# First layer of a four-layer network on one core: six causal turns in a context step, rows turned per tile, block counts within the last routing, the rare blocks' branch in front

## The chip, the cores and the metric

The kernel runs as one program on 1 NeuronCore of a Trainium2 chip. The metric is the device time of one execution in microseconds (us), as a median of several runs. Beside the timed runs one execution is profiled; every reading of the trace below is from that one.

The engines are called as the profile calls them: PE (TensorE) multiplies and transposes into PSUM, DVE (VectorE) and ACT (ScalarE) work on PSUM and SBUF, POOL (GpSimd) does small elementwise work and issues the indirect transfers, SP issues the plain transfers. Each engine works through its own queue in order.

## The reference, cut to what matters

The network has four layers, all in float32, for `x` of 16 sequences of 64 tokens of 256 features (1024 tokens, eight tiles of 128) and a context of 1024 tokens of 192 features for each sequence. Each layer is a cross-attention to the context, a second mixer, and a feed-forward part, each added to `x` after a layer norm. The change touches the first layer alone:

```
x = x + L0_xattn(_layernorm(x), ctx, ctx, ...)       # cross-attention, one head
x = x + L0_attn(_layernorm(x), w_qkv, ln_w, w_proj)  # causal self-attention, 16 heads of 16
x = x + L0_ffn(_layernorm(x), gate_w, w1, w2, w3, sw1, sw2, sw3)

def L0_ffn(x, ...):                # 8 experts, the two largest of each token
    scores = softmax(x @ gate_w.T)
    topk_w, topk_i = top_k(scores, 2)
    y = sum over the two experts of weight * (silu(x @ w1[e]) * (x @ w3[e])) @ w2[e]
    return y + (silu(x @ sw1) * (x @ sw3)) @ sw2      # the shared part, all tokens
```

## The kernel before, in words

**Cross-attention and causal attention together.** `L0_first` walks over the eight tiles of 128 tokens in context steps, `for n in range(NT + 2)`. In step n it does the scores of tile n against its two sequences' contexts (L338; softmax at L222 and L224), the transposes of the exponentials of tile n-1 (L234) and its weighted averages over the context (L349, called `averaged`), and the output of tile n-2 (`by_features` at L357 and L358, `output` with `add_to_x` at L88). The order of PE in this stage is written by hand (`manual_schedule` on PE); the order of the other engines is made by the tile scheduler.

Between those pieces stand calls of `attn.go()`, the causal turns. Each call moves every causal tile at work one `yield` further. A causal tile (`tile(i)`) is a generator of about twenty such pieces: norm (`os`), transpose and eviction (`hTs`, L178), q, k and v (L68 on `hTs`), transposes of q and k (L721), scores `sc` (L68), softmax (DVE L745, L751 and L754, POOL L752, ACT L753), transposes (L760), averages `o` (L782), `sel` and `yT`, projection and addition to `x`. A tile can begin when the cross-attention of that tile is done, three turns after the one before it, and when one of three rooms (buffers) is free; two more rooms come from the context buffers after the last step. In the kernel before there are four turns in a context step. What is left after the last step is done in a loop, `while attn.go(): next(shared, None)`, in which one piece of the shared expert part follows each turn.

**PSUM.** `misc` has two banks in rotation for nearly all small products, `t` two for transposes (and, in this stage, for the shared part's `gu`), and `sc` two double banks, used by the context scores, by the causal scores (two at a time) and by the causal averages `o`.

**Routing.** After two causal tiles, `routing(g)` for that pair goes into the queue `behind`, of which only the first is at work: two layer norms into `htok`, rows written to HBM (`keep_row`, L1155), transposes into `hT` (L178), gate product (`hT` with `gate_w`, L68), then `route`: softmax (L1100 is its exponential on ACT), two largest, ranks (`t_both`, `ahead`), places, and the products of `s_col` and `s_who` into the routing table.

**Experts.** `L0_ffn` first runs `block_experts` (it counts the blocks of 128 routed rows of each expert, computes the list of each block's rows and tokens, and loads `n_blocks` into registers of all engines) between the pieces of the fourth shared part, and then `some_blocks`. There are 23 blocks at most, and 18 are written as plain code (`few`); the other five stand in a branch, `with self.tc.If(self.n_blocks > few)`, behind the 18. In the profiled execution the branch's body is not run. A block gathers its expert's weights `wa` and `wb` and its tokens' rows `hb` with indirect transfers issued by POOL (L1399, three buffers each, the first three of each asked for ahead of the loop), transposes `hb` (L178), multiplies (L68 into `gu` and `po`), and writes its result to `ys` in HBM (L1420, and the transfer at L1421 issued by ACT).

**The next layer's start.** `L1_xattn` needs `ys`: for each tile POOL gathers two `back` tiles (L1399) and DVE adds them to `x` (L1408), and only then come norm and queries (`o` at L894, transposed at L178). Keys and values of the first context (L930 to L951) need none of it.

## Time and profile before

| what | value |
| --- | --- |
| median of the 3 timed runs | 2840.32 us (2838.4 to 2840.79) |
| the profiled execution's own time | 2832.74 us |
| its span, first to last instruction | 2830.9 us |
| mean granted PE clock | 0.964 |
| PE busy | 2601.9 us (92% of the span), 18116 instructions |
| DVE, ACT and POOL busy | 1401.8, 1005.9 and 311.4 us |
| first layer's stages in the profiled execution | start to 42.4 us; steps 2 to 8 from 42.4 to 143.4; the rest of causal attention, routing and shared part to 276.7; expert blocks to 424.0 |

A line of a timeline gives start, duration (us), engine, line and operation, output and inputs, shape, and the number of merged instructions; square brackets hold the engine's idle time before it and what ended that. A line of windows gives each engine's busy time in one stretch, then the granted PE clock as a share of full speed, the DMA engines' share and GB/s. A busy PE is not a PE at its peak: at a lower granted clock the same matmuls show as more busy time.

### The profile page before, as it was taken

Reading aid. Unit: us, or ns where it says so; the run is one execution under the profiler, and the core shown is the slowest. Engines: PE = TensorE matmul, PEld = TensorE weight load, DVE = VectorE, ACT = ScalarE, POOL = GpSimd, SP = SyncE. Lnnn points to the kernel's source line nnn. Section 1 sums busy time; section 2 is a strip of 40 time slices with the busy share of each in tenths; the row PEclk is TensorE's granted clock in tenths of the full one; section 3 lists DMA queues with packets and bytes.
Section 4 is the critical chain, followed back from the end, with each engine's and each line's share of the span. In section 5 each row is a group of like instructions: output and inputs, shape, how many; then the busy total and the mean of one; then the engine's idle time right before and its main releaser. Section 6 shows DMA issues by size and latency. Waiting matters only on the chain.

```text
span 2830.9 us, 44725 instructions
## 1 busy us (share of the span) xinstructions
PE 2601.9 (92%) x18116; PEld 1890.9 (67%) x18116; DVE 1401.8 (50%) x2825; ACT 1005.9 (36%) x2116; POOL 311.4 (11%) x429
## 2 busy tenths in 40 slices
PE   7887998999999898979999999798999998998998
PEld 3566894666666687856666676695666665666777
DVE  3565126666666643233434342423344756658692
ACT  2341223555555431223232222122235445545330
POOL 1121423000000112310101000201001000000000
PEclk9987998999999998989999999799999999999999
DMA  9602862001001015801111112463113213121210
GB/s 268 194 27 83 346 239 67 27 27 39 27 27 35 31 38 193 291 23 49 58 61 51 45 49 87 155 237 108 51 49 94 84 49 96 56 76 31 62 44 8
DMA packets 78156, 253.70 MB, mean 90 GB/s; under 512 B 14079, under 2 KB 25882, under 8 KB 68218
## 3 DMA queue, kind: packets, MB, share of 16 engines
q1 hardware_dynamic: 58490, 165.00, 18.3%
q0 software_dynamic: 13312, 80.28, 7.8%
q10 hardware_dynamic: 6144, 5.51, 0.6%
q8 instruction: 145, 2.38, 0.4%
q14 instruction: 65, 0.53, 0.1%
HBM read 233.80 MB, written 14.81 MB: 88 GB/s over the span
## 4 chain that ended last, share of the span: by engine, by line
PE 39%; DVE 9%; ACT 3%; DMA 2%; issue 2%; POOL 1%; SPq 1%; ACTq 0%; DVEq 0%; POOLq 0%
PE sc L506 9%; PE ps_h L68 5%; PE misc L542 4%; PE halves L68 3%; PE misc L68 3%; PE ps_t L520 3%; PE halves L542 2%; PE gu L68 2%; PE misc L537 2%; PE halves L2136 2%; DVE x L2112 2%; DVE nmx L222 1%; PE halves L537 1%; PE po L68 1%; DMA rep<-dus 1%
## 5 line engine op out<-in xcount | busy, mean ns | idle before, releaser
L222 DVE TENSOR_REDUCE nmx<-sc 128x1 f32<-128x1024 f32 x264 | 311.9, 1219 | 232.1 <-PE sc L506 148.8
L224 ACT ACTIVATE p<-sc,nmx 128x1024 f32<-128x1024 f32 x264 | 294.0, 1114 | 315.3 <-DVE nmx L222 315.3
L506 PE MATMUL sc<-ctxT,qp 128*128 128x512 f32 (+1 forms) x1024 | 360.3, 606 | 0.0
L506 PEld LDWEIGHTS sc<-ctxT,qp 128*128 128x128 f32 (+1 forms) x1024 | 140.7, 191 | 156.9 <-issue 153.8
L520 PE MATMUL ps_t<-ident,p 128*128 128x128 f32 x1024 | 141.3, 281 | 39.7 <-ACT pT L523 16.8
L2102 ACT ACTIVATE da<-rep,al 128x252 f32<-128x252 f32 x256 | 115.7, 499 | 132.3 <-DVE x L2112 122.4
L520 PEld LDWEIGHTS ps_t<-ident,p 128*128 128x128 f32 x1024 | 116.5, 143 | 64.3 <-ACT pT L523 20.0
L2112 DVE TENSOR_TENSOR_SCAN x<-da,x 128x512 f32<-128x512 f32 x128 | 153.0, 1222 | 2.7 <-ACT da L2102 1.9
L234 PE MATMUL misc<-ident,p 128*128 128x128 f32 x1024 | 137.1, 279 | 7.2 <-ACT p L224 6.8
L523 ACT COPY pT<-ps_t 128x512 f32<-128x512 f32 x166 | 94.1, 586 | 122.3 <-PE ps_t L520 122.2
L234 PEld LDWEIGHTS misc<-ident,p 128*128 128x128 f32 x1024 | 110.1, 141 | 32.6 <-ACT p L224 15.1
L159 POOL TENSOR_TENSOR ln_rs<-ln_ve,nhalf 128x1 f32<-128x1 f32 x80 | 44.9, 567 | 679.6 <-DVE ln_ve L157 574.7
L542 PE MATMUL halves<-pT,ctx 128*128 128x256 f32 x512 | 119.5, 387 | 0.0
L542 PE MATMUL misc<-pT,ctx 128*128 128x256 f32 x512 | 119.1, 386 | 0.0
L236 ACT COPY pT<-misc 128x512 f32<-128x512 f32 x128 | 74.9, 585 | 109.0 <-PE misc L234 108.3
L68 PE MATMUL ps_h<-r,w 128*128 128x256 f32 x512 | 113.4, 381 | 0.0
L2108 DVE TENSOR_TENSOR x<-rep,bc_rep 128x512 f32<-128x512 f32 x128 | 84.9, 690 | 56.0 <-PE halves L2136 53.6
L238 DVE COPY pT<-misc 128x512 f32<-128x512 f32 x128 | 88.4, 690 | 39.6 <-PE misc L234 28.5
L68 PEld LDWEIGHTS ps_h<-r,w 128*128 128x128 f32 x512 | 96.6, 190 | 15.9 <-issue 2.5
L542 PEld LDWEIGHTS halves<-pT,ctx 128*128 128x128 f32 x512 | 95.0, 190 | 17.3 <-issue 5.6
L542 PEld LDWEIGHTS misc<-pT,ctx 128*128 128x128 f32 x512 | 94.7, 190 | 17.0 <-issue 5.5
L68 PE MATMUL po<-wb,hid 128*128 128x256 f32 x440 | 100.3, 379 | 0.0
(515 smaller groups left out, 4501.4 us busy)
## 6 DMA issues: line engine op xcount, KB each, us to landing
ctx<-in_ctx SPq DMA_DIRECT2D x48, 768.0 KB
ctxT<-in_ctxT SPq DMA_DIRECT2D x48, 512.0 KB
w<-in_L2f_W SPq DMA_DIRECT2D x24, 1024.0 KB
rep<-dus SPq DMA_DIRECT2D x256, 64.0 KB
ctxT<-in_ctxT SPq DMA_DIRECT2D x16, 768.0 KB
ctxT<-in_ctxT SPq DMA_DIRECT2D x96, 128.0 KB
ys<-yb ACTq DMA_DIRECT2D x40, 128.0 KB
bc_rep<-bcs SPq DMA_DIRECT2D x32, 128.0 KB
```

The source lines that it names most:

```text
L68: self.nc.tensor.matmul(out, lhsT, rhs, start=n == 0, stop=n == len(pairs) - 1)
L222: self.nc.vector.tensor_reduce(nmx, sc, AX.X, ALU.max, negate=True)
L224: self.nc.scalar.activation(p, sc, AF.Exp, bias=nmx, accum_out=sums)
L234: self.nc.tensor.transpose(ps[:, u, :], p[:, at : at + 128], self.ident)
L238: self.nc.vector.tensor_copy(pT[:, 0:4, :], ps)
L506: nc.tensor.matmul(sc[u][:, bass.ts(kh, 512)], qp[n][par][rows, h : h + 2, :].rearrange("p h q -> p (h q)"), ctx[0][rows, at], start=n == ...
L520: nc.tensor.transpose(ps[:, t, :], p[:, at : at + 128], self.ident)
L523: nc.scalar.copy(to, ps)
L537: nc.tensor.matmul(o2[cols, :].rearrange("p (u q) -> p u q", u=2), ck[:, t, 128:], pT[:, t, :, cols], start=t == 0, stop=t == NK - 1,)
L542: nc.tensor.matmul(o, ck[:, t, :128], pT[:, t].rearrange("p u q -> p (u q)"), start=t == 0, stop=t == NK - 1)
L2102: nc.scalar.activation(da[:, g, :, 1:], now[j][:, 0, :].rearrange("p (b s) -> p b s", s=S)[:, :, 1:], AF.Exp, scale=al[:, col : col + 1],)
L2112: nc.vector.tensor_tensor_scan(flat, da.rearrange("p g b s -> p (g b s)"), flat, 0.0, ALU.mult, ALU.add)
```

## The change

It has four parts, all in the first layer.

1. Two more calls of `attn.go()` in a context step: one right after the scores, one in the middle of the averages.
2. The norm, the write of the rows and the transpose that `routing(g)` did for a pair of tiles are done at the end of each causal tile; `routing(g)` begins with the gate product.
3. The two halves of `block_experts` are done inside the last `routing`: the first half after the ranks, the second at its end. All four shared parts run in `L0_first`; the third and the fourth may begin when the last routing has begun, and two pieces of them follow a turn once no causal tile is at work. `L0_ffn` no longer does any of this.
4. The branch with the five rare blocks stands ahead of the 18 plain ones (`rare_first=True`), in the first layer only.

```diff
@@ averaged, and the context steps
+                    if t == NK // 2 - 1:
+                        attn.go()
...
                 got = (n, *scores(n)) if n < NT else None
+                attn.go()
                 if tail is not None:
                     onT = by_features(tail[1])
...
             def parts():
-                for k in range(3):
-                    while attn.turned < (1, 2, NC)[k]:
+                for k in range(NC):
+                    while attn.turned < (1, 2, NC, NC)[k]:
                         yield
                     yield from self.shared_part(k)
...
             while attn.go():
-                next(shared, None)
+                for _ in range(1 if attn.work else 2):
+                    next(shared, None)
@@ tile(i), after its projection
             s.rooms.append(room)
+            if not i:
+                self.htok = self.act.tile([128, NT, D], F32, tag="htok", name="htok")
+                self.hT = self.act.tile([128, 2, T], F32, tag="hT", name="hT")
+            normalized(i, self.htok[:, i, :])
+            self.keep_row(i)
+            yield
+            yield
+            self.evict(self.hT[:, :, i * 128 : (i + 1) * 128], self.transposed(self.htok[:, i, :]))
             if i % 2:
                 s.behind.append(routing(i // 2))
             yield
@@ routing(g)
-            (two norms, two keep_row, two yields, two transposes with evictions)
+            s.turned = g + 1
             ps = self.misc([128, 2, E])
             (gate product, as before)
-            s.turned = g + 1
-            for _ in self.route(self.routed, ps, 2 * g):
-                yield
-                yield
+            route = self.route(self.routed, ps, 2 * g)
+            next(route)
+            yield
+            yield
+            next(route)
+            if g == NC - 1:
+                self.experts = self.block_experts(self.routed, L0_BLOCKS)
+                next(self.experts)
+            yield
+            yield
+            next(route, None)
+            yield
+            if g == NC - 1:
+                next(self.experts, None)
@@ L0_ffn
-        with self.tc.manual_schedule(engines={mybir.EngineType.PE}):
-            experts, part = self.block_experts(self.routed, L0_BLOCKS), self.shared_part(NC - 1)
-            next(experts)
-            for _ in range(2):
-                next(part)
-            next(experts, None)
-            for _ in part:
-                pass
...
-        self.some_blocks(block, self.L0_weights, L0_FEW, L0_BLOCKS)
+        self.some_blocks(block, self.L0_weights, L0_FEW, L0_BLOCKS, rare_first=True)
@@ some_blocks, after the first three weights and tokens are asked for
+        def rare():
+            with self.tc.If(self.n_blocks > few):
+                for j in range(few, most):
+                    w = weights(j, "_few")
+                    block(j, tokens(j, "_few"), *w)
+
+        if rare_first:
+            rare()
         for j in range(few):
             w = ws[j] if j < 3 else weights(j)
             block(j, hbs[j] if j < 3 else tokens(j), *w)
-        with self.tc.If(self.n_blocks > few):
-            ...
+        if not rare_first:
+            rare()
```

More of the change, by code (lines that the diff above doesn't have):

```diff
@@ L812, in routing @@
         def routing(g):
-            if not g:
-                self.htok = self.act.tile([128, NT, D], F32, tag="htok", name="htok")
-                self.hT = self.act.tile([128, 2, T], F32, tag="hT", name="hT")
-            for t in range(2):
-                i = 2 * g + t
-                normalized(i, self.htok[:, i, :])
-                self.keep_row(i)
-            for _ in range(2):
-                yield
-            for t in range(2):
-                i = 2 * g + t
-                cols = slice(i * 128, (i + 1) * 128)
-                self.evict(self.hT[:, :, cols], self.transposed(self.htok[:, i, :]))
-                yield
+            s.turned = g + 1
             ps = self.misc([128, 2, E])
@@ L830, in routing @@
                 self.mm(ps[:, t, :], [(self.hT[:, c, cols], self.gate_w[:, c, :]) for c in range(2)])
-            s.turned = g + 1
-            for _ in self.route(self.routed, ps, 2 * g):
-                yield
-                yield
+            route = self.route(self.routed, ps, 2 * g)
[12 more added lines that the diff above has]
+                next(self.experts, None)
         def go():
@@ L1246, in L0_ffn @@
         self.hid_tag, self.hid_bufs = "hid1", 3
-        with self.tc.manual_schedule(engines={mybir.EngineType.PE}):
-            experts, part = self.block_experts(self.routed, L0_BLOCKS), self.shared_part(NC - 1)
-            next(experts)
-            for _ in range(2):
-                next(part)
-            next(experts, None)
-            for _ in part:
-                pass
         self.start_pack(self.at)
@@ L1367, in block_experts, with some_blocks @@
             nc.vector.tensor_copy(to, slot)
-    def some_blocks(self, block, weights, few, most):
+    def some_blocks(self, block, weights, few, most, rare_first=False):
         zero = self.lp.tile([128, D], F32, tag="yb", bufs=3, name="zero")
@@ L1387, in some_blocks @@
             block(j, hbs[j] if j < 3 else tokens(j), *w)
-        with self.tc.If(self.n_blocks > few):
-            for j in range(few, most):
-                w = weights(j, "_few")
-                block(j, tokens(j, "_few"), *w)
+        if not rare_first:
+            rare()
     def gathered(self, tag, src, at, j):
```

## The prediction

> **What bounds the kernel now.** I read the windows of the first layer first, since nothing else is touched; then the timeline of the context steps, the drain behind them and the block stage's two ends; last PE's and POOL's instruction order in the changed kernel as built, unrun.

> The windows hold steps 2 to 8, the rest up to the first block, the blocks, and the next layer's start:

> ```profile
> 42.40:143.40 101.00, 88.30 (x728) 53.62 (x725) 46.71 (x118) 31.18 (x76) 14.46 (x25) 1.00 0.72 215
> 143.40:276.70 133.30, 108.31 (x744) 81.48 (x742) 83.92 (x332) 43.47 (x89) 23.24 (x29) 0.82 0.12 42
> 276.70:424.00 147.30, 142.39 (x1044) 133.11 (x1044) 29.35 (x81) 32.87 (x98) 48.88 (x66) 1.00 0.79 296
> 424.00:448.00 24.00, 14.98 (x41) 6.62 (x42) 9.88 (x31) 2.81 (x6) 13.94 (x19) 0.82 0.24 68
> ```

> PE is busy 88.3 of 101 us in the steps, with 12.7 of waits, at full clock. In the rest the clock is 0.82, so 108.31 busy us are about 108.31 x 0.82 = 89 us of full-speed work in 133.3: this stage is bound by waits. The blocks are nearly all PE and lack nothing. So the change can win in the second window, if work moves out of it at a smaller price in the first.

> One step, from the timeline:

> ```profile
> 84.79 3.66 PE L338 MATMUL sc<-ctxT,qp 96*64 96x512 f32 x16 [0.78 <-DVE sm L745]
> 89.35 1.22 DVE L222 TENSOR_REDUCE nmx<-sc 128x1 f32<-128x1024 f32 x1
> 90.60 1.11 ACT L224 ACTIVATE p<-sc,nmx 128x1024 f32<-128x1024 f32 x1 [0.52 <-DVE nmx L222]
> ...
> 99.54 1.12 PE L68 MATMUL sc<-w 32*128 32x64 f32 x32
> ...
> 101.44 1.08 PE L338 MATMUL sc<-ctxT,qp 96*64 96x512 f32 x4 [0.78 <-DVE sm L745]
> ```

> A step starts at L338, so this one is 101.44 - 84.79 = 16.65 long. The context scores hold `sc` until ACT's `p`. The causal scores stand late here, just ahead of the next context scores, and the only wait on `sc` is 0.78.

> The drain, and how little idle time slows PE:

> ```profile
> 185.36 1.12 PE L68 MATMUL sc<-w 32*128 32x64 f32 x32
> ...
> 192.43 0.38 PE L773 MATMUL misc<-ident,r 128*8 128x128 f32 x2 [1.87 <-ACT ctx L715]
> ...
> 196.18 1.99 PE L68 MATMUL sc<-ctxT 32*128 32x64 f32 x32
> ...
> 207.16 1.28 ACT L1234 ACT_TABLE_LOAD   x1
> ...
> 244.00 1.13 PE L178 MATMUL misc<-ident,htok 128*128 128x128 f32 x4
> ```

> The same 32 matmuls take 1.12 and, after a 1.87 wait, 1.99. ACT loads tables between the shared part's and the softmaxes' functions.

> The two ends of the block stage:

> ```profile
> 271.50 0.95 POOL L1399 DMA_INDIRECT hb<-hs,tokens  x1 [1.84 <-DVE tokens L1350]
> ...
> 276.73 0.77 PE L178 MATMUL misc<-ident,hb 128*128 128x128 f32 x4 [0.87 <-DMA hb<-hs,tokens]
> ...
> 421.24 2.76 PE L68 MATMUL po<-wb,hid 128*128 128x256 f32 x12
> ...
> 426.80 0.33 POOL L655 IOTA of<- 8x256 int32 x1 [24.90 <-PEq L1388]
> ...
> 427.98 1.10 PE L68 MATMUL misc<-w,bv 128*128 128x256 f32 x4 [3.98 <-DVE bv L882]
> 428.38 0.96 POOL L1399 DMA_INDIRECT back<-ys,route_at  x1 [0.17 <-issue]
> ...
> 430.08 3.78 PE L930 MATMUL misc<-ctxT,w 128*128 128x512 f32 x4
> ...
> 439.32 1.98 PE L930 MATMUL misc<-ctxT,w 128*128 128x512 f32 x4
> ...
> 447.19 0.66 PE L178 MATMUL misc<-ident,o 128*128 128x128 f32 x2 [4.83 <-DVE o L894]
> ```

> Before, the first `hb` takes 276.73 - 271.50 = 5.23 from issue to use, under shared matmuls; PE waits 0.87. At the end every engine meets at the branch: POOL waits for PE's sequencer until 426.80, though PE's last instruction was issued by 424. PE stands 3.98, and the gap leaves it slow (3.78 for four matmuls that later take 1.98). What ends the 4.83 at 447.19 is the chain `back`, `xs`, norm, `o`.

> **Part 1, six turns.** Full-speed PE work, summed from rows like these: a context step 9.05 (scores 3.6, `on` 0.45, transposes 1.05, output 1.1, averages 2.8); a causal tile 8.45 (q, k, v 2.75, scores 1.1, transposes 1.0 and others). In the changed order tiles 0 to 4 are through by step 8 and two more under way (before: 0 to 2), so steps 2 to 8 hold 9.05, 12.5, 14.6, 17.7, 18.2, 19.4 and 14.4, sum 105.9 against 88.3: 17.6 us move in.

> What is new there: a causal `sc` stands directly behind the context scores and wants both double banks. One comes free when `p` is done: 1.22 for `nmx` and 1.11 for `p`, with starts, 2.4 us after the scores; 0.7 of small products covers some of it. Behind that wait stand `on`, `sel` and all the rest of PE's queue. The next q, k and v then wait for a `misc` bank that DVE frees only behind two `sm` (0.69), two `mx` (0.68), `onT` (0.28) and `yT` (0.42). Step 5, from its start: scores to 3.65, `r` and `o` to 4.4, wait 1.8, `sc` to 7.3, `on` and `sel` to 8.9, wait 2.0, q/k/v to 13.7, transposes, output, `yT` and `pT` to 17.4, averages with the tiles' transposes 21.4. That is 17.7 of work and 3.7 of waits.

> So laid out, steps 2 to 8 take 12.1, 15.5, 19.0, 21.4, 22, 24 and 18, together 132.0 (before 12.1, 15.3, 15.0, 16.6, 14.8, 13.2, 14.0). Bounds: 118.6, if only the 12.7 of waits of before remain (105.9 + 12.7), and 140, if each step loses another 1 to 1.5 to the clock. I take 132, since both waits have rows.

> **Parts 2 and 3, the rest.** Work left: 88.3 + 89 - 105.9 = 71. At the share of before, 133.3 / 89 = 1.50, that takes 106.5. The reordered shared parts bring ACT from 11 table loads to 5 in this stage: 6 x 1.28 = 7.7, of which I count 5, since ACT is idle half the stage and PE doesn't meet each load. Turning rows per tile ends the queueing seen at the last pair, whose rows are normalized at 235.85 and transposed at 244.00; the rest must still run gate, ranks, block list and rows in a chain through DVE, while the shared parts give cover. Norm and write per tile add no instruction; SP's `keep_row` goes earlier in a queue with slack (DMA share 0.12 here). Estimate 101.5; bounds 90 (all 7.7 and the 8 us gone) and 110 (fewer tiles at once, no load on the path).

> Steps and rest: 132.0 + 101.5 = 233.5, against 101 + 133.3 - 0.87 = 233.4. **The interleaving comes to 0**, from -13 (118.6 + 101.5) to +8 (140 + 101.5).

> **Part 4, the branch in front.** In the changed order POOL asks for the first `wa` and `wb`, then meets the branch, and only then asks for `hb`, although the code names `hb` earlier. The branch waits for all engines, and DVE reaches it behind its last addition of the shared part. Price, after PE's last shared matmul: that addition 0.8, the branch 2.05 (DVE's and PE's last work ends at 424.77 at the latest, POOL runs on at 426.80), then `hb` 5.23: 8.1 against 0.87, **+7.2**. Nothing covers it: all four shared parts are over. Floor 4.4 (5.23 - 0.87: addition and branch lie under other work), ceiling 9 (the branch meeting one more engine late). PE then starts slow: (3.78 - 1.98) from above, and 0.95 for the following four matmuls of L932 (2.08 at 433.79 against 1.13 at 441.24): **+2.7**, from 0.6 to 3. The branch's body is not run. The 147.3 of the blocks stay.

> At the stage's end the meeting is gone. PE goes from the last `po` straight to `bv` and the keys, but the end is set by 447.19, so by the first `back`. POOL can ask for it when the last `ys` has landed; its iota and memsets (1.4 in all) run ahead of that. Before it asked at 428.38. ACT wrote the last `yb` by 424.40 and issued `ys` until 424.77; with about 2 us to land, 426.8, the gain is 1.6: **-1.6**, from 0 (the transfer was the cause before as well) to -3.6 (it lands at once). What is then late next is the same chain on DVE.

> On the clock the trace shows a wait of 1.87 followed by half-speed rows, so a step's two waits of about 2 can cost more than themselves; the forecast takes no such loss, as the wait of 0.78 left 3.66 at full speed. [...]

> For the branch, the row (2.05) decides. [...]

> **Sum.** 0 + 7.2 + 2.7 - 1.6 = +8.3. On the profiled execution (2832.74) that is 2841.0; its own time is 7.6 under the median, and on the median 2840.32 it gives 2848.6.

> **Rivals.** The measurement tells 0.2% from no change, 5.7 us either way: faster is below 2834.6, slower above 2846.0.

> Faster: *the longer turns hide the waits.* Tiles at different pieces fill each other's waits, so the steps keep 12.7 (118.6), and the rest is 98 to 102. For it: DVE, the releaser of both waits, is busy under half of the steps (46.71 of 101). Against: PE's order is fixed, so no work can pass a waiting `sc`. With the rest at 98 (all 7.7 of the loads gone) interleaving gives (118.6 + 98) - 233.4 = -17, the sum -17 + 8.3, or 2832; with the branch and its slow rows at their floors, 4.4 + 0.6 - 1.6 = 3.4, it is 2827. It decides once a step's waits average 2.2 instead of 3.7: 7 x 1.5 and 3.5 from the rest are 14, which pays the 8.3 and the 5.7 below.

> No change: part of the waits hidden, or `back` up to 3.6 earlier and the `hb` gap at 5 rather than 8.1: -2 to -6 against the forecast, about 2842.

> Clock: each of seven steps loses 1 to 1.5 after its waits, as at 196.18 (0.87 on one group): +8, 2857.

> That parts 2 and 3 do nothing is covered by the rest at 106.5: 2854.

> **How the numbers follow.** Forecast 0.38 (2846 to 2854), clock 0.18, no change 0.16, faster 0.28. Slower 0.38 + 0.18 = 0.56. The range 2829 to 2861 leaves out the best of the faster case and the worst of the clock case, some 0.18 together.

> **What would show it.** In the changed profile: L338 starts 19 to 24 us apart in steps 4 to 7, each `sc` wait after the scores ended by `p`; the last shared matmul near 276; POOL's first `hb` behind the branch and an idle PE of about 8 us ahead of the first `hb` transposes, then slow rows; blocks of 147 to 150; `bv` directly behind the last `po`, the first `back` about 1.6 us sooner after it; 5 table loads in the drain. Wrong: steps under 17 us, `hb` asked for before the last shared matmul, or granted clock under 1.00 in the steps.

## The result, and the profile after

The changed kernel takes 2849.93 us (median of 6 runs, 2849.58 to 2852.78), the kernel before 2839.36 in the 6 runs counted with it: a difference of the medians of +10.6 us. The ratio of the means is 1.0042, with a 95% interval of 1.0029 to 1.0055. The forecast was 2848.6, +8.3 on the median shown then.

The windows of the changed kernel, cut at its own stages: steps 2 to 8; the rest up to the last shared matmul; the gap to the first block; the 18 blocks; the way to the next layer's first `o`. The columns are as before (busy time of PE, PEld, DVE, ACT and POOL, granted PE clock, DMA share, GB/s):

```profile
42.53:183.30 140.77, 123.75 (x908) 74.95 (x905) 69.57 (x196) 41.01 (x101) 20.15 (x32) 0.88 0.51 155
183.30:287.40 104.10, 84.28 (x565) 65.08 (x564) 60.73 (x253) 26.79 (x58) 13.46 (x18) 0.84 0.12 43
287.40:295.49 8.09, 0.00 (x0) 0.03 (x1) 0.42 (x1) 0.00 (x0) 5.66 (x6) 0.63 0.87 264
295.49:443.56 148.07, 143.87 (x1045) 135.09 (x1046) 30.72 (x89) 32.49 (x98) 47.49 (x65) 0.99 0.77 287
443.56:464.64 21.08, 12.21 (x39) 5.68 (x38) 7.38 (x21) 2.70 (x5) 12.31 (x17) 0.90 0.26 77
```

The first trace of before was a short one: 2832.74 for its execution against a median of 2839 to 2840. A second trace of the same kernel (2839.79, the first experiment) is the fairer measure. Its windows, cut in the same way, are 108.21, 131.01, 0.72, 147.82 and 23.80 us; the first two of them:

```profile
42.52:150.73 108.21, 94.95 (x730) 56.21 (x727) 46.69 (x118) 31.22 (x76) 14.49 (x25) 0.94 0.66 201
150.73:281.74 131.01, 106.82 (x743) 80.43 (x742) 83.65 (x331) 43.52 (x89) 22.74 (x28) 0.83 0.12 41
```

So the changed kernel has 32.6 more in the steps, 26.9 less in the rest, 7.4 more in the gap, 0.3 more in the blocks and 2.7 less at the end: +10.6 (with rounding), the difference of the medians.

Steps 4 to 8 one by one, the changed kernel again:

```profile
74.43:94.26 19.83, 16.37 (x117) 9.96 (x117) 9.18 (x21) 6.61 (x16) 3.39 (x5) 0.91 0.72 199
94.26:117.08 22.82, 20.59 (x163) 12.78 (x162) 11.80 (x30) 7.29 (x17) 3.91 (x6) 0.85 0.47 145
117.08:140.96 23.88, 21.96 (x173) 14.30 (x172) 12.00 (x30) 7.55 (x18) 3.91 (x6) 0.86 0.44 141
140.96:164.09 23.13, 20.18 (x168) 12.35 (x167) 17.80 (x71) 6.38 (x17) 3.92 (x6) 0.93 0.17 70
164.09:183.30 19.21, 17.93 (x151) 12.58 (x150) 9.85 (x25) 6.45 (x16) 3.03 (x4) 0.82 0.24 86
```

Look at the clock: 0.82 to 0.93 in each of them, where the two traces of before had 1.00 and 0.94 over all their steps. Idle time is only 1.3 to 3.5 us a step. What makes a step long is seen in step 5, on PE's timeline:

```profile
100.51 1.22 PE L68 MATMUL sc<-w 32*128 32x64 f32 x32 [1.68 <-ACT p L224]
...
102.14 2.07 PE L68 MATMUL misc<-rT,sel 8*128 8x128 f32 x8
104.72 4.78 PE L68 MATMUL misc<-w,hTs 128*128 128x512 f32 x8 [0.52 <-DVE yT L803]
```

The wait of `sc` on `p` is there as forecast (1.68). But behind it `sel` takes 2.07 (1.15 at full speed) and q, k and v 4.78 (2.75): some 3 us that no wait explains.

The start of the blocks, timeline of all engines:

```profile
287.43 0.34 SPq L1538 DMA_DIRECT2D w<-in_L1a_conv  x1
287.44 0.42 DVE L88 TENSOR_TENSOR xs<-xs,misc 128x256 f32<-128x256 f32 x1 [1.57 <-PE misc L68]
287.87 0.38 SPq L1374 DMA_DIRECT2D ys<-zero  x1
288.06 0.95 POOL L1407 DMA_INDIRECT hb<-hs,tokens  x1 [8.00 <-DVEq L1388]
...
295.49 0.66 PE L178 MATMUL misc<-ident,hb 128*128 128x128 f32 x2 [8.09 <-DMA hb<-hs,tokens]
```

The gap is the forecast 8.1, but made of other pieces: DVE's last addition ends 0.46 after PE, POOL asks for `hb` 0.20 after that, and `hb` takes 7.43 to arrive.

To compare kernels I split PE's time in the steps and the rest into work (busy time x granted clock), waits (length less busy time) and slow time (busy time x (1 - clock)). Busy time grows as the clock falls: q, k and v take 2.75 at 1.00, and 5.49 at 0.50 in the run with large fillers below. The clock has two digits, so work and slow time are good to about 1 us.

| kernel, profiled execution | steps + rest | work | waits | slow time |
| --- | --- | --- | --- | --- |
| before, first trace | 233.5 | 177.1 | 36.9 | 19.5 |
| before, second trace | 239.2 | 177.9 | 37.4 | 23.9 |
| changed | 244.9 | 179.7 | 36.8 | 28.3 |
| the two turns alone | 252.7 | 179.2 | 38.9 | 34.7 |
| the other parts, no new turns, branch behind | 234.3 | 178.7 | 35.2 | 20.4 |

The turns moved work and waits about, and against the second trace of before neither grew by more than 2 us; they added slow time. Beside the traces, the mean granted clock of each timed run is on record (it counts PE's idle time too: the gap of the changed kernel, with no matmul in it, stands at 0.63 above). With the two turns alone its mean over six runs is 0.9588, against 0.9626 over the 29 runs of before counted with them. As an estimate, that is 0.0038 x 2840 = 10.8 us of their +12.1. So the lower clock is not only a matter of the one execution that was profiled.

### The profile page after: what moved, and what is told of

The parts are those of the page before. It is cut to its first block, busy times and chain, and to the rows that moved or that the text cites. A ratio compares the mean times of both kernels' runs of the same rounds, so it can differ in the third digit from the quotient of the medians.

```text
span 2848.4 us, 44713 instructions
## 1 busy us (share of the span) xinstructions
PE 2615.1 (92%) x18116; PEld 1899.6 (67%) x18116; DVE 1401.3 (49%) x2825; ACT 998.6 (35%) x2110; POOL 310.7 (11%) x429
## 3 DMA queue, kind: packets, MB, share of 16 engines
q1 hardware_dynamic: 58490, 165.00, 18.2%
## 4 chain that ended last, share of the span: by engine, by line
PE 40%; DVE 9%; ACT 3%; issue 2%; DMA 2%; POOL 1%; SPq 1%; DVEq 0%; ACTq 0%; POOLq 0%
PE sc L510 9%; PE ps_h L68 5%; PE misc L546 4%; PE halves L68 3%; PE misc L68 3%; PE ps_t L524 3%; PE gu L68 2%; PE halves L546 2%; PE misc L541 2%; DVE x L2120 2%; PE halves L2144 2%; DVE nmx L222 1%; PE halves L541 1%; PE po L68 1%; DVE x L2116 1%
## 5 line engine op out<-in xcount | busy, mean ns | idle before, releaser
L222 DVE TENSOR_REDUCE nmx<-sc 128x1 f32<-128x1024 f32 x264 | 311.9, 1219 | 246.3 <-PE sc L510 150.3
L224 ACT ACTIVATE p<-sc,nmx 128x1024 f32<-128x1024 f32 x264 | 294.0, 1114 | 331.7 <-DVE nmx L222 331.5
L524 PE MATMUL ps_t<-ident,p 128*128 128x128 f32 x1024 | 141.7, 281 | 38.4 <-ACT pT L527 17.0
L234 PEld LDWEIGHTS misc<-ident,p 128*128 128x128 f32 x1024 | 110.1, 141 | 32.9 <-ACT p L224 15.3
L68 PE MATMUL ps_h<-r,w 128*128 128x256 f32 x512 | 113.4, 381 | 0.0
L238 DVE COPY pT<-misc 128x512 f32<-128x512 f32 x128 | 88.3, 690 | 40.0 <-PE misc L234 29.0
L68 PEld LDWEIGHTS ps_h<-r,w 128*128 128x128 f32 x512 | 96.7, 190 | 15.8 <-issue 2.5
L68 PE MATMUL po<-wb,hid 128*128 128x256 f32 x440 | 100.4, 379 | 0.0
```

Of the source, the lines that this page charges most:

```text
L68: self.nc.tensor.matmul(out, lhsT, rhs, start=n == 0, stop=n == len(pairs) - 1)
L222: self.nc.vector.tensor_reduce(nmx, sc, AX.X, ALU.max, negate=True)
L224: self.nc.scalar.activation(p, sc, AF.Exp, bias=nmx, accum_out=sums)
L234: self.nc.tensor.transpose(ps[:, u, :], p[:, at : at + 128], self.ident)
L238: self.nc.vector.tensor_copy(pT[:, 0:4, :], ps)
L524: nc.tensor.transpose(ps[:, t, :], p[:, at : at + 128], self.ident)
```

## The experiments

**The kernel before again**, unchanged, for a second trace.

> The kernel before, unchanged, for a second profile. The first profiled execution took 2832.74, 7.6 under its median, while the changed kernel's profiled execution (2850.2) lies on its own median; so the two traces differ by 17.5 and the medians by 10.6. If the first trace of before was a lucky execution, this trace has a span of 2835 to 2840 and is longer than 2830.9 at a place that can be named; if the first trace is what before does in its steps and drain, the first layer again ends its last shared matmul at 276 and the difference lies in later layers.

Its median is 2838.89 and its span 2838.0. The first layer is 6.9 longer than in the first trace (its `o` at 454.08 against 447.19), and 5.7 of that lies in the steps and the rest, 4.4 of them slow time. Step 3 alone, second trace:

```profile
54.94:73.97 19.03, 15.87 (x73) 7.60 (x75) 4.16 (x11) 3.92 (x11) 1.35 (x3) 0.82 0.78 217
```

In the first trace that step took 15.33 at full clock. So the first trace was a lucky execution, as the first theory has it, and what differs can be named: PE's clock.

**The branch in front alone.** `L0_ffn` of before calls `some_blocks(..., rare_first=True)`, nothing else.

> Before with the branch ahead of the 18 blocks and nothing else. Theory of the prediction: PE idle about 8 us ahead of the first hb transposes (0.87 before), and 1.6 to 2 back at the end of the blocks; in all +6 to +8, median 2845 to 2848. Rival: the long gap in the changed kernel came with the block counts within the routing (the hb transfer there shares the queues with the write of zeros to ys and the next layer's weights, issued at the same moment); then the branch alone costs its 0.2 and one 5.2 landing, +3 to +5, 2842 to 2845.

2837.68 against 2838.91, ratio 1.0000 (0.9990 to 1.0009): no cost, and both expectations missed. Its timeline:

```profile
280.99 0.94 POOL L1406 DMA_INDIRECT hb<-hs,tokens  x1 [4.45 <-remote]
...
281.49 0.87 PE L178 MATMUL misc<-ident,hb 128*128 128x128 f32 x4 [2.79 <-PEq L1387]
```

Here POOL had asked for two `hb` at 274.34 and 275.59, ahead of the branch; only the third stands behind it. PE loses 2.79 at the branch itself, and gains 2.5 at the end of the blocks (21.29 against 23.80). What the forecast charged to the branch, a whole transfer without cover, needs `hb` to stand behind it.

**The two turns alone.** Before with `attn.go()` after the scores and in the middle of the averages.

> Before with the two new causal turns and nothing else. Theory of the steps: the waits of about 2 us on the exponentials behind each context score, and the half-speed q, k and v behind them, make steps 2 to 8 about 35 us longer, and the rest is shorter by less: +4 to +10, median 2844 to 2850. Rival, the drain: the turns win what they move and the loss lies in the routing turned per tile and the counts within it; then this is 0 to -8, 2832 to 2840.

2851.04, +12.1, ratio 1.0046 (1.0031 to 1.0061), just above the range of the theory of the steps. The whole loss is in the turns. Its steps and rest:

```profile
42.51:189.12 146.61, 127.59 (x906) 77.95 (x903) 68.19 (x196) 40.80 (x100) 20.26 (x32) 0.85 0.49 149
189.12:295.17 106.05, 86.22 (x567) 66.17 (x568) 61.42 (x253) 27.14 (x59) 16.89 (x22) 0.82 0.14 51
```

Steps +38.4, rest -25.0 against the second trace of before: +13.4, of which 10.8 are slow time, 1.5 waits and 1.3 work.

**The change without its turns.** The two added calls are taken out of the changed kernel.

> The changed kernel without its two new turns (four in a step), all else as changed. Theory of the steps: steps as before (101 us from 42.4 to the last averages, at full clock), the branch's +6 and a drain with five table loads in place of eleven: +2 to +6, 2841 to 2845. Rival, the drain: no better than the changed kernel, 2848 to 2856.

2840.3, +1.4, ratio 1.0006 (0.9996 to 1.0016), just under the range expected. Steps and rest are 234.3, but the first `hb` comes 4.57 after the last shared matmul, and PE then waits 3.24 for the second. The steps are not at full clock as expected (108.22 us at 0.95), but neither are those of the second trace of before (108.21 at 0.94).

**The branch back behind the blocks**, in the changed kernel: `rare_first=True` dropped.

> The changed kernel with the branch back behind the 18 blocks; its instruction order still has POOL's first hb wait for the sequencers of all engines, since n_blocks is loaded ahead of it. Theory of the branch: the 8.09 of idle PE ahead of the first hb transposes falls to about 1, the end of the blocks is 2.7 longer again; the median is 2844 to 2846, 5 under the changed kernel. Rival, the early counts: the gap is the meeting of the engines at the load of n_blocks together with the zeros and weights that SP sends at that moment, and stays at 6 to 8; the median is 2850 to 2853.

2850.47, ratio 1.0049 (1.0033 to 1.0065) against 1.0042 for the changed kernel: no difference. The time is the rival's. The gap, 5.32 without a branch, lies between the two theories (about 1, and 6 to 8):

```profile
292.57 0.66 PE L178 MATMUL misc<-ident,hb 128*128 128x128 f32 x2 [5.32 <-DMA hb<-hs,tokens]
```

POOL asked for this `hb` at 287.19, 0.87 earlier than in the changed kernel and 0.1 ahead of SP's weights and zeros instead of behind them; it took 5.4 to arrive instead of 7.4. The blocks behind it took 2.4 longer and the end 0.9 longer, so nothing was won.

**Parts 2 and 3 alone**: the change without its turns, branch behind.

> Parts 2 and 3 alone: four turns, the branch behind. Theory of the branch: last shared matmul as in the run without the new turns (277, against 282 in the second trace of before), hb gap about 1: -3 to -5, median 2834 to 2836, faster than both kernels. Rival, the early counts: the gap stays at 4 to 8 and eats the gain, 2838 to 2842.

2838.15, +1.3, ratio 1.0004 (0.9992 to 1.0016). Here the rival holds, in time and gap: steps and rest are 4.9 shorter than in the second trace of before, and the gap (5.62) and the blocks (150.4 against 147.8) take it back. Timeline at the end of the rest:

```profile
275.37 0.17 DVE L1348 CAST tokens<-misc 128x23 int32<-128x23 f32 x1
275.51 1.57 PE L68 MATMUL misc<-w,hid 128*128 128x256 f32 x6 [0.18 <-DVE xs L88]
277.02 0.95 POOL L1404 DMA_INDIRECT hb<-hs,tokens  x1 [8.16 <-issue]
```

The tokens are ready 1.5 us before PE's last shared matmul ends, instead of 4.6 in the first trace of before (271.23 against 275.86), and `hb` is asked for another 1.5 later, when the engines have loaded `n_blocks`, whose buffer it takes over.

**Six turns, one moved.** In the changed kernel the call after the scores goes, and the averages hold two:

```diff
-                attn.go()            # after the scores
-                    if t == NK // 2 - 1:
+                    if t in (NK // 4 - 1, 3 * NK // 4 - 1):
```

> The changed kernel with six turns still, but the one behind the scores moved into the averages (turns after a quarter and after three quarters of them, none in the middle). In the built order the causal sc then stands just ahead of the context scores, as in the kernel before, while q, k and v still stand behind the transposes of on. If the place behind the scores is what costs (waits on p of about 2 in each step, then half speed): steps shorten by 2 to 3 each, -8 to -14 under the changed kernel, median 2836 to 2842. If it is the amount in a step, whatever its place (DVE and ACT serve too many tiles at once): within 3 of the changed kernel, 2847 to 2853.

2850.33, +13.5, ratio 1.0055 (1.0040 to 1.0071). The time is that of the theory of the amount, and most of the waits on `p` are gone (1.0 us in the steps, 5.6 in the changed kernel). But the trace doesn't fit that theory. Its steps, and step 5's q, k and v:

```profile
41.39:172.74 131.35, 115.29 (x917) 68.84 (x913) 70.36 (x200) 41.66 (x102) 20.93 (x33) 0.97 0.56 167
...
96.82 2.85 PE L68 MATMUL misc<-w,hTs 128*128 128x512 f32 x8 [1.25 <-DVE yT L802]
```

The steps are 9.4 shorter than in the changed kernel, with 3.5 of slow time instead of 14.8, and q, k and v are at full speed in steps 5 and 6 (4.4 to 4.5 in 7 and 8), much as the theory of the place has it. The next layer's `o` comes 7.1 earlier (457.59 against 464.64), but the later layers, which no edit touched, take 2388.3 us instead of 2383.8. This execution, 2847.7, was the shortest of the kernel's six, so one trace doesn't settle it: over the six runs the move won nothing, and what the place behind the scores costs stays open.

**One new turn**: before with the call in the averages alone.

> Before with the new turn in the averages alone, five turns in a step. Theory of the place: no wait on p, so no loss: 2834 to 2841. Theory of the amount: half of the loss of the run with both turns (+12.1), 2843 to 2847.

2846.67, +9.8, ratio 1.0037 (1.0023 to 1.0051): the time lies in the range of the theory of the amount, but one turn costs most of what two do (9.8 of 12.1), not half. The theory of the place fails here: without a turn behind the scores the loss is there. The trace puts only 3.6 of it in front of the next layer's `o` (457.71 against 454.08), 3.7 more in later layers, which no edit touched. Those layers take between 2383.2 and 2388.3 us in the fourteen traces, whatever the edit, so a single trace places a loss of this size poorly.

**Filling the wait with small products.** The changed kernel, with the averages `o` of tiles 0 to 3 computed three times:

```diff
-            for c in range(2):
+            for c in list(range(2)) * (3 if i < 4 else 1):
```

> The changed kernel with more work on PE: the causal averages o of tiles 0 to 3 are computed three times over (the same products into the same place, 2 x 0.67 us of PE more for each of the four tiles, 5.4 in all), which in four of the steps stand directly ahead of the causal sc that waits 1.7 for p. Theory of the clock: the wait leaves PE at half speed from about 2 us after it (q, k and v 4.8 to 5.2 in place of 2.75, sel 2.07 in place of 1.15); with the wait filled, those rows are at full speed, steps 5 to 8 are 2 to 3 shorter each, the granted clock in the steps is above 0.93 (0.88), and the time falls by 4 to 10 to 2840 to 2846 although work was added. Rival: the half-speed rows have another cause, or the waits themselves are the loss; then the added work shows in part, 2850 to 2856.

2854.85, +16.2, ratio 1.0057 (1.0042 to 1.0071): the rival. The waits on `p` fell to 0.75 and 0.73 in steps 5 and 6, a wait of 0.88 for DVE's `ym` took part of their place, and q, k and v still took 4.5 to 5.5. In step 5 the stretch behind the scores, then q, k and v:

```profile
97.50:101.00 3.50, 1.87 (x34) 1.73 (x32) 1.16 (x4) 0.73 (x2) 0.00 (x0) 0.83 0.89 222
102.00:108.00 6.00, 5.49 (x13) 3.24 (x13) 3.80 (x8) 1.41 (x3) 2.14 (x3) 0.50 0.36 91
```

**Filling it with large products.** At the same place four full products a tile, overwritten by `o`:

```diff
+            for _ in range(4 if i < 4 else 0):
+                nc.tensor.matmul(o[:, 0, :], wqkv[:, 0, :128], wqkv[:, 0, :512], start=True, stop=True)
```

> The changed kernel with a filler at the same place as in the run before (ahead of the averages o of tiles 0 to 3), but of another kind: four products of a full 128 x 128 weight with 512 columns (about 0.34 us each at full speed, 1.37 a tile, 5.5 in all), written into o's own place and overwritten by o. In the traces the half-speed rows come 4 to 5 us after the last large product, at the end of a stretch of small ones (r with 8 rows, o and sc on 32 x 64 pieces, on, sel) and of the waits between them; the filler of small products left them as they were. Theory: products that use little of the array don't hold the clock, and a large one does; then q, k and v behind the stretch come back from 4.5 to 5.5 towards 2.75 in steps 5 to 8, slow time in the steps falls from 15 to under 8, and the time is 2843 to 2849, 6 to 12 under the filler of small products (2854.85). Rival: whatever fills the wait, the clock falls; slow time in the steps stays at 13 to 17 and the time is 2852 to 2857.

2863.37, +25.2, ratio 1.0091 (1.0074 to 1.0108). Both expectations missed. The price was mis-sized: a tile's four products are eight records of 0.45 on the trace, 3.60 in all and not 1.37 (0.34 is an eighth of the 2.75 of q, k and v, eight records of the same shape), so 14.4 for the four tiles, which is the whole distance to the changed kernel (13.4). Step 5: the filler, the small products behind it, then q, k and v:

```profile
94.70:98.30 3.60, 3.60 (x12) 1.40 (x10) 1.37 (x2) 1.56 (x3) 0.00 (x0) 1.00 0.78 268
98.30:104.30 6.00, 3.57 (x75) 2.86 (x74) 4.08 (x9) 0.00 (x0) 1.14 (x3) 0.90 0.78 195
104.40:109.80 5.40, 5.40 (x9) 2.87 (x10) 1.80 (x4) 2.29 (x7) 1.28 (x2) 0.50 0.01 2
```

The fall of the clock moved behind the filler, and `sel` came back to 1.15. But the clock fell again at about 103.1, by the 0.90 of the second of these rows: in the 4.7 us from the end of the filler PE was busy 3.57, with one wait of 1.02 for `ym`. Slow time in the steps is 10.6 (14.8 in the changed kernel): a part of the theory's effect, no proof of it, and not worth its price.

**More cover for the first tokens.** Parts 2 and 3 alone, with one piece of the shared parts a turn to the end, and `n_blocks` in a buffer of its own:

```diff
-                for _ in range(1 if attn.work else 2):
-                    next(shared, None)
+                next(shared, None)
-        n = self.lp.tile([1, 1], I32, name="n_blocks")
+        n = self.routes.tile([1, 1], I32, tag="n_blocks", name="n_blocks")
```

> Parts 2 and 3 alone (four turns, branch behind), with two edits: one piece of the shared parts follows each turn to the end, so that in the built order a whole shared part (about 8.7 us) stands behind the product that gives the tokens instead of a third of one; and n_blocks lies in a buffer that hb's does not reuse, so hb no longer waits for the sequencers of all engines. If the lost cover of the hb transfer is what eats the gain of parts 2 and 3 (steps and drain 234.3, against 239.2 in the second trace of before): hb gap about 1, -3 to -6 against before, 2831 to 2836, faster than both kernels. If fewer pieces in the list's waits give the gain back: within 2 of before.

2837.87, ratio 0.9999 (0.9988 to 1.0009). The first `hb` now has its cover (gap 1.08), but the second, transposed right behind it, is waited for 3.47, and the blocks take 152.4 instead of 147.8. The cover was won and the time given back one transfer later. No version beats the kernel before.

**Only the buffer of its own**:

> Parts 2 and 3 alone (four turns, branch behind, up to two pieces a turn as in the change), with n_blocks in a buffer that hb's does not reuse. If the wait for the sequencers is the cause of the late hb: issued directly behind the tokens instead of 1.5 later, gap 4 instead of 5.6, -1 to -2 against the run with the shared buffer. If the place of the tokens' product in PE's order is: no difference over 1.5.

2839.68, ratio 1.0004 (0.9995 to 1.0013). `hb` goes 0.76 after the tokens instead of 1.48 and the gap is 3.21 instead of 5.62, so the wait for `n_blocks` is a cause of the late `hb`, as the first theory says. But the blocks take 152.2 instead of 150.4, the gain of 1 to 2 isn't there, and no time is won that these runs can tell.

## Why the prediction was right, and where not

The number held (2849.93 for 2848.6, between 2829 and 2861) and so did the direction. The reasons held only in part: three terms of the sum missed, by +5.7, -2.4 and -1.1, and partly offset each other. Steps and rest, forecast at 233.5, took 244.9, which is 11.4 more. In the difference it shows as 5.7 only because the second trace of before is itself 5.7 longer there than the one that the sum was worked out from. That the sum still came out at +8.3 for +10.6 is in part luck.

**Part 1, the steps.** The forecast had 105.9 of work and 26.1 of waits, 132.0. Measured: 108.9 of work, 17.0 of waits and 14.8 of slow time, 140.8. The step that failed is the sentence that "the forecast takes no such loss": the waits were charged at half again what they are, and the clock at nothing. One of the prediction's own signs of being wrong, a granted clock under 1.00 in the steps, is there (0.88). The mechanism named as the rival "clock" is there, at 1.4 to 3.2 a step (busy time x (1 - clock) in steps 4 to 8) instead of 1 to 1.5. What brings it isn't the wait on `p` alone, as that rival had it: with the waits moved or filled, the loss of time stayed, though the one trace with the waits moved had little slow time in its steps. What lowers the clock when turns are added stays open.

**Parts 2 and 3.** The rest took 104.1 for 101.5, with five table loads as forecast, but not from the reordered shared parts: the turns alone bring the eleven loads to five, and parts 2 and 3 without the turns only to nine. The sum "interleaving 0" came out at +5.7 against the second trace of before. The runs split it: the turns alone are +12.1, all other parts together +1.4. Without turns, steps and rest are some 5 shorter than in the second trace; this is no more than the spread between the two traces of before (5.7), so its size stays open, and what the earlier rows and the two loads fewer give was not told apart.

**Part 4.** The gap is 8.09 for 8.1, the end -2.7 for -1.6, the slow rows at most 0.3 for 2.7. But the cause was wrong. Alone the branch costs nothing (1.0000), and taking it out of the changed kernel gains nothing. The gap comes from the tokens, which are ready late against PE's last shared matmul (in parts 2 and 3 alone, with a whole shared part behind the tokens' product and `n_blocks` in its own buffer, it was 1.08), and from the loads of `n_blocks` (5.62 with the shared buffer, 3.21 without). A third cause is possible: SP begins to send 1280 KB of weights and 640 KB of zeros in the same microsecond; in the first trace of before the zeros went at 236.29. That SP's transfers lengthen `hb` (5.4 when `hb` goes 0.1 ahead of them, 7.4 when it goes 0.6 behind) was seen in two traces and not tested by moving them, and the 5.23 of the first trace of before, with `hb` 4.4 ahead of the weights, doesn't fit so simple a rule.

The 2.05 charged for the branch was the price of a register load, a branch and the meeting of the engines together: in that trace ACT's load of `n_blocks` (0.47) stands directly ahead of its branch, whose record takes 0.045 there, as on POOL and SP (0.072 on DVE; PE's, 3.75, begins under its last matmuls), and POOL goes on 1.4 later. Where `n_blocks` is loaded before, as in the changed kernel, POOL goes on 0.20 after DVE's last addition; with the branch in front alone PE loses 2.79, addition and meeting of the engines included. In the first trace of before, where all engines but PE load `n_blocks` just ahead of the branch, a load takes 0.47 to 0.54. The 2 us that the prediction gives the last `ys` to land has a row further on in that trace: a `ys` that ACT issued until 1215.17 released POOL's next gather at 1217.48, 2.31 later.

**The rivals.** "The longer turns hide the waits" was half right: the waits did not grow (36.8 for 37.4 with 1.8 more of work; 17.0 in the steps, 2.4 in each, near the 2.2 at which that rival was to win), and yet it was slower. A wait count alone would have given no change.

## What to carry to other kernels

Before moving small products between waits, read the granted clock of the stage beside its idle time: with the two turns, work and waits grew by under 3 us and slow time by 11. When a sum is right, test its terms one by one; here the turns alone gave the whole loss, and the branch, which was charged with it, cost nothing alone. And compare traces only after a second trace of the same kernel: two executions of before differ by 5.7 us in the stage that was changed.
